# A two-layer kernel whose second layer begins inside the first layer's plan, with its first transfers planned and another table of due times

## The chip, the cores and the metric

One Trainium2 chip, one of its cores. The metric is the device time of one launch in microseconds (us). The kernel before ran three times: 2150.53, 2154.84 and 2156.69 us, median 2154.84.

## The reference

Both layers work on x of 32 sequences x 128 tokens x 512 numbers, in float32. Layer 0 is a cross attention with grouped heads (32 query heads of 16 numbers, 8 key and value heads) over a context, then a residual and a norm:

```python
q, k, v = hidden @ Wq + bq, context @ Wk + bk, context @ Wv + bv
scores = einsum("bkgld,bksd->bkgls", q, k) * scale + mask
out = einsum("bkgls,bksd->bkgld", softmax(scores), v)
x = out @ Wo + bo + hidden
x = (x - mean(x)) * rsqrt(var(x) + EPS) * gamma + beta
```

Layer 1 is a recurrent layer: its inputs are mixtures of each token with the one before (the first with a row of the context), its decay depends on the data, and its state of 16 x 16 numbers per head runs along the tokens:

```python
xn = ln(x); sx = token_shift(xn, state[:, 1])
xxx = tanh((xn + sx * maa_x) @ maa_w1)              # five parts of 32
x5 = xn + sx * (maa_stack + xxx @ maa_w2)           # w, k, v, r, g
w = exp(-exp(time_decay + tanh(x5[w] @ decay_w1) @ decay_w2))
r, k, v, g = x5[r] @ Wr.T, x5[k] @ Wk.T, x5[v] @ Wv.T, silu(x5[g] @ Wg.T)
for each token: out = r . (u * k v + s);  s = k v + w * s
att = head_norm(out) * gn_w + gn_b
x = x + att * g @ Wo.T
xn2 = ln(x); xk, xr = xn2 + sx2 * ffn_maa_k, xn2 + sx2 * ffn_maa_r
x = x + sigmoid(xr @ fWr.T) * (square(relu(xk @ fWk.T)) @ fWv.T)
```

## The kernel before

**Groups.** Each layer goes through the 32 sequences in 16 groups of two. Layer 0 has one function for a group, attend. Layer 1 has four: load1 (the group's rows and its start state), front (norm, mixtures, projections), recurrence (the scan along the tokens) and tail (the output projection and the feed-forward half). x between the layers goes through DRAM (x1d), in 256 KB tiles.

**The plan.** Nothing is issued in the order in which it is written. Each call of add makes a step: an engine, an estimate of its work, a function that issues its instructions, and the tiles (cells) that it reads and writes. A table (WHEN0 for layer 0, WHEN1 for layer 1) gives each kind of step a due time in units of groups; the step's due is its group plus that entry. give_out is a list scheduler: it models the engines' free times, and at each turn issues the step that can begin first and, among those that begin within 0.3 us, the one that is due first. A step may not run more than a set number of groups ahead of the oldest step that isn't issued (15.2739 in layer 0, 13.2672 in layer 1). A cell takes a place in a pool of few buffers at its first write; a place comes free when all uses of its cell are issued (`_places`). In layer 1 a further rule, turns, holds that the cells of one pool take their places in the order of their due times; in layer 0 it is off. What comes out is a fixed order for each engine: PE, DVE, ACT, POOL, and SP, whose queue carries most DMAs. Within an engine all is in order, DMA issues and their waits too.

**The two plans.** Layer 0's plan is given out in full; then the weights of layer 1 are loaded from ACT's queue (L726 to L763) and the constants made; then layer 1's plan begins, with pools of its own. The first transfers are outside the plan: ident and col, then on SP wk, wv, bk, ev, bv_bc, three row_bc and prev (L433 to L450), on ACT's queue wq and wo, all in the order of the program, ahead of the first x, ct and mask (L490 to L498).

**Layer 0, one group**, by the names of tiles: x is transposed (pxT L506, xT L512) and projected (pq L557); the context, loaded already transposed (ct), gives pk (L530) and pv (L583). Scores sc (L613), mask and softmax (pr L629, mx L641, exps L653), transposes ppT (L665) with copies pT (L670, L672), po (L677). The row sums go out to DRAM and come back spread over partitions (rs, rT, rd L701, bc L707), and scale oT (L711). pw (L716) is the output projection, then residual, norm and store of x1d (L719 to L724).

**Layer 1, one group.** load1 fetches x1t and s0 (L988). front: norm and transposes (zt L415, pxnt L860, xnt L868), the mixture xx (L905), ph0 (L924) and its tanh h0 (L1009); px5 (L1025) for two of five mixtures at a time, finished on DVE (L1041) and POOL (L1055); pdd (L1090), which needs the mixture w, with hd (L1095); pk and pv (L938), copied to kx and vx (L1071); v goes to DRAM (vd L1105) to be fetched spread (kv L1230); pr, pg, and the decay pew (L1162), ew (L1172). recurrence: POOL multiplies (L1252), DVE scans (a L1267) and multiplies by r (ar L1281), PE sums over the key index (acc L1296, pd L1207, pc L1321), and takes the variance pvar (L1344). tail: rstd (L1350) is spread by pb (L1357), pwo, the second norm with pxnc (L860), pkk, pkv, prr and the store. The feed-forward weights fk and fr are fetched anew for each group (L1400).

In PSUM, tiles of one bank (tag g) serve most of PE's results, three places in each layer. pdd's instructions, which pack four products of 32 rows, stand in one step:

```python
        for c in range(KC):
            for i, w, src in ((0, wd1[:, c, 0:32], xw), (1, wd1[:, c, 32:64], xw),
                              (2, w1[:, c, P:160], xx), (3, w1[:, c, P:160], xx)):
                nc.tensor.matmul(pdd()[32 * i : 32 * i + 32, :N], w, flat(src()[:, c]), ...)
```

The main loop issues nothing; it fills the plan: front of group 0, then for each group front of the next, recurrence, tail.

Of the kernel before, what the change touches and what calls it, by code (L numbers as in the profile page):

```python
# [8 lines left out]
F32 = mybir.dt.float32  # L9
# [5 lines left out]
P = 128  # L15
B = 32
# [19 lines left out]
        oT 0: -2.6252, oT 1: 3.3357, pT 0 0 0: -0.1744, pT 0 1 0: 1.2267, pT 1 0 0: -1.9192, pT 1 1 0: -0.8740,  # L36
        pr 0 0 0 0: 0.6529, pr 0 0 0 1: -0.0746, pr 0 0 1 0: -4.0682, pr 0 0 1 1: -0.1561, pr 0 1 0 0: 0.4501,
        pr 0 1 0 1: -0.3203, pr 0 1 1 0: -0.7878, pr 0 1 1 1: 0.0820, pr 1 0 0 0: 1.7871, pr 1 0 0 1: 2.2002,
        pr 1 0 1 0: -0.8730, pr 1 0 1 1: -1.8966, pr 1 1 0 0: -0.4270, pr 1 1 0 1: -2.0592, pr 1 1 1 0: 3.7724,
        pr 1 1 1 1: -0.8531, qT 0: -0.5042, qT 1: -0.0255, qT 2: -0.2635, qT 3: -1.0961, xT 0: 0.4768, xT 1: -0.1677  # L40
    """,
    "DVE": """
        kT 0: 1.2690, kT 1: -3.2473, mx 0 0 0: -1.1417, mx 0 0 1: -0.2864, mx 0 1 0: 1.2620, mx 0 1 1: -2.6166,
        mx 1 0 0: 2.6711, mx 1 0 1: -0.5335, mx 1 1 0: 1.7226, mx 1 1 1: -0.3724, pT 0 0 1: -1.2967, pT 0 0 2: 0.0513,
        pT 0 0 3: 0.0848, pT 0 1 1: -8.6724, pT 0 1 2: 0.0095, pT 0 1 3: -0.9150, pT 1 0 1: 0.2278, pT 1 0 2: 1.5335,
        pT 1 0 3: 0.1265, pT 1 1 1: -0.6521, pT 1 1 2: 0.0264, pT 1 1 3: -1.1512, pprev: -0.5247, pr 0 0 0: 3.0552,
        pr 0 0 1: -0.2034, pr 0 1 0: -6.8992, pr 0 1 1: 0.0841, pr 1 0 0: 3.8180, pr 1 0 1: 5.4106, pr 1 1 0: -0.1859,
        pr 1 1 1: -1.0387, pv: 1.4494, rT 0: 1.7614, rT 1: -6.4827, rs 0: 0.0025, rs 1: -1.3038, st a 0: 3.4819,
        st a 1: -0.7930, x 0: -1.6215, x 1: -0.7745
    """,  # L50
    "PE": """
        pk: -1.2090, po 0 0: -0.9547, po 0 1: -1.2559, po 1 0: 1.2553, po 1 1: -6.5573, ppT 0 0 0: -3.2574,
        ppT 0 0 1: -3.1897, ppT 0 0 2: 0.0759, ppT 0 0 3: -0.0050, ppT 0 1 0: -5.1850, ppT 0 1 1: -1.0390,
        ppT 0 1 2: -1.3378, ppT 0 1 3: -0.1908, ppT 1 0 0: -0.7659, ppT 1 0 1: 0.2863, ppT 1 0 2: -2.6538,
        ppT 1 0 3: -0.7327, ppT 1 1 0: -1.0396, ppT 1 1 1: -1.1030, ppT 1 1 2: -1.7141, ppT 1 1 3: -1.3304,
        pprev: 0.5587, pq 0: -0.5900, pq 2: -0.5203, pv: -0.7591, pw 0: -0.0622, pw 1: 0.0036, pxT 0: -1.1551,
        pxT 1: -1.2087, sc 0 0: -0.4025, sc 0 1: -0.1903, sc 1 0: 0.0128, sc 1 1: 0.3141
    """,
    "POOL": """
        oT 0: 1.2881, oT 1: 3.1556, sd a 0: -1.3405, sd a 1: -6.4837, x 0: -1.9469, x 1: 2.5134, z 0: -5.8626,  # L60
        z 1: -2.1882
    """,
    "SP": """
        bc 0: -0.4187, bc 1: -0.5237, ct 0: -1.3394, ct 1: -1.7142, m 0: -0.3457, m 1: 0.1999, rd 0: -8.2177,
        rd 1: 2.2127, x 0: -1.7606, x 1: -2.6917, z 0: 0.8576, z 1: -0.5330
# [4 lines left out]
        att 0: 8.9413, att 1: 10.3245, att 2: 10.9514, att 3: 4.2202, ew 0: 3.0530, ew 1: 7.1294, ew 2: 5.4799,  # L70
        ew 3: -0.1804, gt 0: 2.7896, gt 2: 7.2564, h0: 4.2793, hd: -0.7228, kk 0: 1.5652, kk 2: 8.9401,
        kv 0 0 0: 2.8237, kv 0 0 1: 2.8350, kv 0 1 0: 6.5988, kv 0 1 1: 4.7931, kv 1 0 0: 11.5248, kv 1 0 1: 12.1370,
        kv 1 1 0: 8.1713, kv 1 1 1: 8.4770, kv 2 0 0: 11.3074, kv 2 0 1: 0.7816, kv 2 1 0: 10.6862, kv 2 1 1: 7.1872,
        kv 3 0 0: 19.3264, kv 3 0 1: 5.1004, kv 3 1 0: 5.3317, kv 3 1 1: 6.5296, pk 0: 7.8527, pk 2: 3.7734,
        pv 0: 2.8655, pv 2: 13.4147, r 0: 10.0348, r 2: -0.1824, rr 0: 13.0999, rr 1: 2.8864, rstd: 5.6019,
        sq 0: -0.0986, sq 1: 8.8327, sq 2: 0.5974, sq 3: 5.6588, w4 0: 6.7771, w4 1: 3.1835, w4 2: 6.2518,
        w4 3: 1.3276, xnc 0: 5.1909, xnc 1: 3.5402, xnc 2: 5.5512, xnc 3: 9.4093, xnt 0: 4.3436, xnt 1: 6.3722,
        xnt 2: 7.1367, xnt 3: 8.6670, xx 0: 11.9355, xx 1: 6.5413, xx 2: 5.6875, xx 3: 9.8818, yk 0: 11.1356,
        yk 1: 1.7804, yk 2: 15.8112, yk 3: 13.9956, yr 0: 7.4657, yr 1: 8.8095, yr 2: 3.2938, yr 3: 8.7878,
        zc 0: 7.6581, zc 1: 0.9023, zt 0: 10.9657, zt 1: 5.2637  # L80
    """,
    "DVE": """
        a 0 0: -0.5883, a 0 1: -0.2414, a 0 2: 0.1043, a 0 3: 8.0118, a 1 0: 7.0047, a 1 1: 12.1762, a 1 2: 5.6912,
        a 1 3: 9.0685, a 2 0: 9.3322, a 2 1: 6.5083, a 2 2: 6.9110, a 2 3: 0.9712, a 3 0: 7.3177, a 3 1: 7.6874,
        a 3 2: 2.3097, a 3 3: 12.5406, ar 0 0: 2.4656, ar 0 1: 9.7666, ar 0 2: 5.7906, ar 0 3: 7.9178, ar 1 0: 6.6300,
        ar 1 1: 1.2202, ar 1 2: 6.5895, ar 1 3: 8.7855, ar 2 0: 28.3612, ar 2 1: 16.5392, ar 2 2: 12.3754,
        ar 2 3: 11.7973, ar 3 0: 9.1129, ar 3 1: 12.3189, ar 3 2: 9.0665, ar 3 3: 1.8400, gn 0: 8.4672, gn 1: 5.8193,
        gn 2: 3.6790, gn 3: 6.5194, gt 0: 0.0430, gt 2: -0.3529, own 0: 7.8602, own 1: 10.0300, own 2: 6.6987,
        own 3: 5.2960, pb 0: 0.7953, pb 1: 8.4093, pb 2: 4.1923, pb 3: 8.8563, raw 0: 2.2489, raw 1: 0.4033,
        raw 2: 5.9725, raw 3: 6.8204, rk 0: -0.4021, rk 1: 1.1444, rr 0: 7.1091, rr 1: 5.2378, rstd: 2.3485,  # L90
        st c 0: 6.9368, st c 1: 1.2521, st t 0: 8.7646, st t 1: 7.8543, x1c 0: 1.0294, x1c 1: 6.6954, x5 0 0: 2.9930,
        x5 0 1: 7.2539, x5 0 2: -1.0976, x5 0 3: 11.6924, x5 1 0: 8.4707, x5 1 1: -0.2943, x5 1 2: 10.2532,
        x5 1 3: 6.3221, x5 2 0: -0.6575, x5 2 1: 6.4713, x5 2 2: 12.8297, x5 2 3: 15.9903, x5 3 0: 6.5967,
        x5 3 1: 6.3600, x5 3 2: -0.8402, x5 3 3: -0.6696, x5 4 0: 8.4589, x5 4 1: 12.8956, x5 4 2: -0.4045,
        x5 4 3: 5.3981
    """,
    "PE": """
        acc 0: 13.3710, acc 1: 6.5427, acc 2: 6.5657, acc 3: 5.8187, pb 0: 18.0159, pb 2: 13.4697, pc 0: 0.6934,
        pc 1: 3.6234, pc 2: 5.2455, pc 3: 6.5762, pd 0: 1.0255, pd 1: 5.0703, pd 2: 6.9998, pd 3: 6.9286, pdd: 8.4674,
        pew 0: 6.2963, pew 2: 8.3876, pg 0: 1.2658, pg 2: 11.7555, ph0: 5.5651, pk 0: -0.5984, pk 2: -0.5853,  # L100
        pkk 0: 6.0318, pkk 2: 6.3700, pkv 0: 3.8400, pkv 1: 1.5996, pr 0: 0.4302, pr 2: -0.2452, prr 0: 3.2418,
        prr 1: 6.5661, pv 0: 20.6763, pv 2: -0.4713, pvar: 9.0706, pwo 0: 6.3422, pwo 1: 7.2520, px5 1 0: 6.5332,
# [226 lines left out]
def xattn_rwkv_kernel(  # L329
# [91 lines left out]
    with ExitStack() as sa:  # L421
# [8 lines left out]
        for tag in ("ln_st", "ln_mv", "ln_sd"):  # L430
            pl.tag(tag, 2)
# [1093 lines left out]
```

## Time and profile before

| what | us |
|---|---|
| median of three runs | 2154.84 |
| the profiled execution | 2150.95 |
| its span | 2149.2 |
| PE busy, in the span | 1992.6 |
| one steady group of layer 0 (between two pxT) | 35.72 |
| one steady group of layer 1 (between two pk) | 88.7 |
| last pvar to the end | 56.8 |

Busy times are sums over instructions; the four compute engines and the DMA queues run side by side, tied by semaphores, so a share of 93% says that PE works nearly always, not that it works at full clock. The granted clock of PE, 0.962 of full in the mean, is given for each stretch. The costliest groups of instructions (line, engine, operation, tiles; busy time, mean ns of one; idle time of the engine before them and what ended most of it):

```profile
L1252 POOL TENSOR_TENSOR kv<-kv,kx 128x1016 f32<-128x1016 f32 x256 | 597.6, 2349 | 142.9 <-DMA kv<-vd 63.1
L1267 DVE TENSOR_TENSOR_SCAN a<-w,kv 128x1024 f32<-128x1024 f32 x256 | 587.3, 2294 | 29.1 <-ACT w L1191 8.0
L653 ACT ACTIVATE pr<-pr,mx 128x128 f32<-128x128 f32 x1024 | 398.3, 391 | 53.4 <-DVE mx L641 47.0
L1281 DVE TENSOR_TENSOR ar<-a,r 128x1024 f32<-128x1024 f32 x256 | 311.5, 1217 | 4.4
```

### The profile page before, as it was taken

Reading aid. Unit: us, or ns where it says so; the run is one execution under the profiler, and the core shown is the slowest. Engines: PE = TensorE matmul, PEld = TensorE weight load, DVE = VectorE, ACT = ScalarE, POOL = GpSimd, SP = SyncE. Lnnn points to the kernel's source line nnn. Section 1 sums busy time; section 2 is a strip of 40 time slices with the busy share of each in tenths; the row PEclk is TensorE's granted clock in tenths of the full one; section 3 lists DMA queues with packets and bytes.
Section 4 is the critical chain, followed back from the end, with each engine's and each line's share of the span. In section 5 each row is a group of like instructions: output and inputs, shape, how many; then the busy total and the mean of one; then the engine's idle time right before and its main releaser. Section 6 shows DMA issues by size and latency. Waiting matters only on the chain.

```text
span 2149.2 us, 36169 instructions
## 1 busy us (share of the span) xinstructions
PE 1992.6 (93%) x11908; PEld 1305.8 (61%) x11908; DVE 1783.0 (83%) x2182; ACT 1058.0 (49%) x3473; POOL 1294.0 (60%) x1081
## 2 busy tenths in 40 slices
PE   5999999999958779999999999999999999999977
PEld 4666666666626546566675665656657566575643
DVE  3888888888844888989988899898988989888881
ACT  3888888888842233433434434344343443433332
POOL 1273334343345666777777777777777877777552
PEclk9999999999978889999999999999999999999988
DMA  7232221221024687887977978879788797886851
GB/s 207 61 127 66 62 70 60 68 61 60 27 81 80 114 121 114 146 158 122 175 122 138 167 117 168 130 138 163 120 161 134 141 165 117 162 136 115 163 99 59
DMA packets 155883, 252.23 MB, mean 117 GB/s; under 512 B 50512, under 2 KB 97648, under 8 KB 139312
## 3 DMA queue, kind: packets, MB, share of 16 engines
q1 hardware_dynamic: 149232, 240.27, 59.8%
q10 hardware_dynamic: 6464, 9.66, 1.4%
q8 instruction: 94, 1.54, 0.4%
q14 instruction: 93, 0.76, 0.1%
HBM read 224.12 MB, written 25.69 MB: 116 GB/s over the span
## 4 chain that ended last, share of the span: by engine, by line
PE 52%; DVE 7%; ACT 2%; DMA 1%; issue 1%; POOL 0%; SPq 0%; POOLq 0%; DVEq 0%; ACTq 0%
PE pkk L938 5%; PE pwo L956 5%; PE pk L938 5%; PE pv L938 5%; PE pr L938 4%; PE acc L1296 4%; PE pkv L956 4%; PE pg L938 4%; PE prr L956 4%; DVE a L1267 3%; PE pdd L1090 2%; PE px L1025 2%; DVE x L1041 2%; PE pc L1321 1%; PE pew L1162 1%
## 5 line engine op out<-in xcount | busy, mean ns | idle before, releaser
L1252 POOL TENSOR_TENSOR kv<-kv,kx 128x1016 f32<-128x1016 f32 x256 | 597.6, 2349 | 142.9 <-DMA kv<-vd 63.1
L1267 DVE TENSOR_TENSOR_SCAN a<-w,kv 128x1024 f32<-128x1024 f32 x256 | 587.3, 2294 | 29.1 <-ACT w L1191 8.0
L653 ACT ACTIVATE pr<-pr,mx 128x128 f32<-128x128 f32 x1024 | 398.3, 391 | 53.4 <-DVE mx L641 47.0
L1281 DVE TENSOR_TENSOR ar<-a,r 128x1024 f32<-128x1024 f32 x256 | 311.5, 1217 | 4.4
L1055 POOL TENSOR_TENSOR x<-x,xnt 128x512 f32<-128x512 f32 x160 | 187.2, 1181 | 92.1 <-DVE x L1041 79.4
L653 ACT ACTIVATION_READ_ACCUMULATOR pr<-pr,mx 128x1 f32 x1024 | 193.7, 189 | 0.0
L1041 DVE SCALAR_TENSOR_TENSOR x<-px,col,sxt 128x256 f32<-128x256 f32 x320 | 133.9, 473 | 59.5 <-PE pdd L1090 37.2
L629 DVE TENSOR_TENSOR pr<-sc,m 128x1024 f32<-128x1024 f32 x128 | 153.7, 1210 | 32.1 <-PE sc L613 29.0
L665 PE MATMUL ppT<-ident,pr 128*128 128x128 f32 x1024 | 154.3, 281 | 12.1 <-DVE pT L672 4.3
L665 PEld LDWEIGHTS ppT<-ident,pr 128*128 128x128 f32 x1024 | 115.4, 141 | 77.9 <-issue 25.9
L641 DVE TENSOR_REDUCE mx<-pr 128x8 f32<-128x1024 f32 x128 | 155.5, 1215 | 2.7
L1296 PE MATMUL acc<-ar,give 128*32 128x256 f32 x2048 | 142.5, 394 | 12.6 <-DVE ar L1281 12.6
L672 DVE COPY pT<-ppT 128x512 f32<-128x512 f32 x192 | 128.3, 682 | 22.9 <-PE ppT L665 18.2
L397 POOL TENSOR_SCALAR sd_a<-mv_a 128x1 f32<-128x1 f32 x32 | 7.1, 223 | 214.6 <-DVE mv_a L393 214.5
L716 PE MATMUL pw<-wo,oT 128*128 128x512 f32 x256 | 122.3, 610 | 9.8 <-POOL oT L711 8.8
L938 PE MATMUL pkk<-yk,fk 128*128 128x256 f32 x512 | 121.4, 392 | 6.2 <-POOL yk L905 6.2
L956 PE MATMUL pwo<-wo,gt 128*128 128x512 f32 x256 | 122.2, 612 | 5.0 <-ACT xnt L868 2.9
L938 PE MATMUL pr<-x,wr 128*128 128x256 f32 x512 | 122.0, 387 | 3.8 <-DVE x L1041 3.8
L557 PE MATMUL pq<-xT,wq 128*128 128x256 f32 x512 | 122.9, 389 | 0.7 <-ACT xT L512 0.7
L938 PE MATMUL pk<-x,wk 128*128 128x256 f32 x512 | 123.3, 390 | 0.0
L956 PE MATMUL pkv<-fv,kk 128*128 128x512 f32 x256 | 120.3, 603 | 0.0
L938 PE MATMUL pg<-x,wg 128*128 128x256 f32 x512 | 117.6, 383 | 2.9 <-DVE x L1041 2.9
(146 smaller groups left out, 3714.7 us busy)
## 6 DMA issues: line engine op xcount, KB each, us to landing
kv<-vd SPq DMA_DIRECT2D x1024, 128.0 KB
fk<-in_fWkT_dram SPq DMA_DIRECT2D x16, 1024.0 KB
fr<-in_fWrT_dram SPq DMA_DIRECT2D x16, 1024.0 KB
x<-in_x_dram SPq DMA_DIRECT2D x32, 256.0 KB
ct<-in_ctxT_dram SPq DMA_DIRECT2D x32, 256.0 KB
bc<-rd SPq DMA_DIRECT2D x256, 32.0 KB
x1d<-z SPq DMA_DIRECT2D x32, 256.0 KB
x1t<-x1d SPq DMA_DIRECT2D x32, 256.0 KB
```

The source lines that it names most:

```text
L629: lambda b=b, sc=sc, jp=jp, pr=pr: nc.vector.tensor_tensor(pr(), sc()[:, 2 * jp : 2 * jp + 2].rearrange("p j g e s -> p (j g e) s"), ms[b] ...
L641: lambda pr=pr, mx=mx: nc.vector.tensor_reduce(mx(), pr(), AX.X, ALU.max, negate=True),
L653: nc.scalar.activation(pr()[:, 4 * i + h, :], pr()[:, 4 * i + h, :], AF.Exp, bias=mx()[:, 4 * i + h : 4 * i + h + 1], accum_out=sm()[:, h0 ...
L665: nc.tensor.transpose(pt()[:, h, :], pr()[:, 4 * i + h, :], ident)
L938: nc.tensor.matmul(pp()[:, i], (w() if isinstance(w, Cell) else w)[:, kc, (c + i) * P : (c + i + 1) * P], flat(src()[:, kc]), start=(kc == 0),
L956: nc.tensor.matmul(pp(), src()[:, c, b, :], (w() if isinstance(w, Cell) else w)[:, c, :], start=(c == 0), stop=(c == KC - 1),)
L1041: lambda i=i, c=c, pp=pp, half=half: nc.vector.scalar_tensor_tensor(flat(ts[i]()[:, c]), pp()[:, half], col[:, MS0 + i, c : c + 1], flat(s ...
L1055: lambda i=i, c2=c2: nc.gpsimd.tensor_add(ts[i]()[:, c2 : c2 + 2].rearrange("p c b t -> p (c b) t"), ts[i]()[:, c2 : c2 + 2].rearrange("p ...
L1252: lambda c=c, kv=kv, e=e: nc.gpsimd.tensor_tensor(kv()[:, e, :, :, 1:T], kv()[:, e, :, :, 1:T], k()[:, c, :, 0 : T - 1].unsqueeze(1).broad ...
L1267: lambda kv=kv, a=a, e=e: nc.vector.tensor_tensor_scan(a().rearrange("p j b t -> p (j b t)"), w4().rearrange("p j b t -> p (j b t)"), kv() ...
L1281: lambda c=c, a=a, ar=ar: nc.vector.tensor_tensor(ar(), a().rearrange("p j b t -> p j (b t)"), flat(r()[:, c]).unsqueeze(1).broadcast_to([ ...
L1296: nc.tensor.matmul(acc()[32 * j : 32 * j + 32, :N], give[:, d].rearrange("p e h -> p (e h)"), tiles[d]()[:, j], start=(d == 0), stop=(d == 3),
```

## The change

The same tiles are computed by the same instructions; where they stand, and in which queues, changes.

1. **One table more than before, none the same.** Both tables are replaced, entry by entry, and so are the bounds on running ahead: 15.2739 becomes 9.8213 in layer 0, 13.2672 becomes 0.7291 in layer 1. Layer 0's table now holds the names of layer 1's front too. add takes a due time that stands where the table has none.
2. **Layer 1's plan is made first,** with the pools that both layers can use (xt, s0, z, xn, sx, x5, h0, hd, the norms' small tiles and the one-bank PSUM tiles g), and layer 0's plan takes them in: ct now lies in sx, prev in z.
3. **front becomes a generator** that stops after hd. For the first group, load1 and that first part of front are put into layer 0's plan; the rest is taken up at the start of layer 1's.
4. **The first transfers are steps of the plan on SP:** wk, wv, wo (before on ACT's queue), bk and ev, bv, row_bc, prev, and as one step w1, wd1, w2, wd2 (before on ACT's queue).
5. **The rule of turns** no longer holds for the one-bank tiles g.
6. **Wv and Wg of layer 1** are reordered through one staging tile of 512 columns in eight steps, before through three of 1024 in four.
7. give_out forgets cells of the plan before whose uses are all issued, and sets the ends of what remains to 3.4.

```diff
+    FREE = ("g",)
-        s.due = s.group + self.when[s.key]
+        s.due = s.group + self.when.get(s.key, due - s.group)
-        if self.turns and any(c.turn - self.begun[c.tag] >= taken[c.tag] for c in fresh):
+        if self.turns and any(c.tag not in self.FREE and c.turn - self.begun[c.tag] >= taken[c.tag] for c in fresh):
     def give_out(self):
+        for _, _, live in self.pools.values():
+            live[:] = [c for c in live if any(u.end is None for _, _, u in c.uses)]
+            for c in live:
+                for _, _, u in c.uses:
+                    u.end = u.end and 3.4
...
+    pl1 = Plan(ctx, tc, WHEN1, 0.7291)
...
-        wt = sa.enter_context(tc.tile_pool(name="wt", bufs=3))
-        pl = Plan(sa, tc, WHEN0, 15.2739)
+        wt = sa.enter_context(tc.tile_pool(name="wt", bufs=1))
+        pl = Plan(sa, tc, WHEN0, 9.8213)
         pl.turns = False
+        pl.pools.update(pl1.pools)
...
         wq = load_w(Wq, E, "wq", wa, nc.scalar)
-        wk = load_w(Wk, P, "wk", wa, nc.sync)
-        wv = load_w(Wv, P, "wv", wa, nc.sync)
-        wo = load_w(Wo0, E, "wo", wa, nc.scalar)
+        def later(name, t, move, go, due):
+            c = Cell(None, None, name, t=t)
+            pl.add("SP", 0.5, go, w=[c], of=f"{name}_0", due=due, move=move)
+            return c
+        def weight(w, width, name, due):
+            t = wa.tile([P, KC, width], F32, name=name)
+            return t, later(name, t, width / 85, lambda: nc.sync.dma_start(t, w.rearrange("(c p) m -> p c m", p=P)), due)
+        wk, wk_c = weight(Wk, P, "wk", -0.9)
+        wv, wv_c = weight(Wv, P, "wv", -0.7)
+        wo, wo_c = weight(Wo0, E, "wo", -0.2)
...
+        bk_c = later("bk", bk_sb, 0.2, small, -0.85)
+        bv_c = later("bv", bv_bc, 0.4, lambda: nc.sync.dma_start(bv_bc, bv.broadcast_to([P, P])), -0.65)
+        row_c = later("rows", row_bc, 4.0, three, -0.1)
+        prev_c = pl.cell("z", [T, E], "prev_0")
+        pl.add("SP", 0.5, lambda: nc.sync.dma_start(prev_c()[: 2 * B], prev), w=[prev_c], due=0.5, move=0.7)
...
-            ct = pl.cell("ct", [P, KC, G, T], f"ct_{gr}")
+            ct = pl.cell("sx", [P, KC, G, T], f"ct_{gr}")
...
         for gr in range(NG):
             attend(gr)
+        w1_c = later("w1", w1, 5.0, first_weights, 2.0)
+        add, cell = pl.add, pl.cell
+        first = load1(0, NG - 2.0)
+        first.w = [w1_c]
+        ahead = front(first, NG - 1.5)
+        next(ahead)
         with tc.manual_schedule():
             pl.give_out()
...
-            for half in range(2):
-                tmp = wt.tile([P, 2, E], F32, tag="wtmp", name=f"wtmp_{n}{half}")
...
+            for c in range(KC):
+                tmp = wt.tile([P, E], F32, tag="wtmp", name=f"wtmp_{n}{c}")
+                nc.scalar.dma_start(tmp, src[c * P : (c + 1) * P])
...
         add("ACT", act(N), lambda: nc.scalar.activation(hd(), pdd()[:, :N], AF.Tanh), r=[pdd], w=[hd], due=D + 0.35)
+        yield
```

In the changed kernel's order of instructions the following stand differently around the steps named above. On SP: ident, col, wk, x_0_0, bk, ev, x_0_1, ct_0, the rows and contexts of groups 1 and 2, m_0_0, row_bc, and then wv, s0, bv, wo, prev, w1 and the rest. On PE, at the end of layer 0: ph0 of layer 1's first group before the last two po, px5 (w and k) on both sides of the last po, then pdd, the last pw, and pk. In layer 1, per group, between the second half of px5 (w and k) and pdd: half of pg, two pxnc and one pd.

## The prediction

> **What bounds the kernel now.** I read the busy shares first, then the 40 slices, then what each engine waited for, then single stretches of time.
>
> ```profile
> span 2149.2 us, 36169 instructions
> PE 1992.6 (93%) x11908; PEld 1305.8 (61%) x11908; DVE 1783.0 (83%) x2182; ACT 1058.0 (49%) x3473; POOL 1294.0 (60%) x1081
> PE   5999999999958779999999999999999999999977
> PEclk9999999999978889999999999999999999999988
> PE 52%; DVE 7%; ACT 2%; DMA 1%; issue 1%; POOL 0%; SPq 0%; POOLq 0%; DVEq 0%; ACTq 0%
> ```
>
> PE is busy 93% of the span and holds the chain that ended last. The slices show the exceptions: the first, and three or four around the twelfth (some 610 to 750 us), where the layers meet. Only there, and in PE's waits inside a group, is there anything to win. The table of PE's waits (us in total, times, longest):
>
> ```profile
> PE pdd L1090 <- DVE x L1041: 29.8, 14, 2.1
> PE pprev L471 <- DMA prev_sb<-in_prev_dram: 16.4, 1, 16.4
> PE pxnt L860 <- ACT zt L415: 13.8, 2, 13.2
> PE acc L1296 <- DVE ar L1281: 12.6, 6, 3.3
> PE ph L924 <- POOL xx L905: 8.9, 2, 5.3
> PE pw L716 <- POOL oT L711: 8.8, 3, 6.8
> ```
>
> One wait recurs (pdd, 14 of 16 groups); one belongs to the start; three belong to the meeting of the layers. That meeting on PE's timeline (start, duration, then in brackets the idle time before):
>
> ```profile
> 611.96 1.07 PE L677 MATMUL po<-pT,v 128*32 128x256 f32 x16
> 619.83 6.53 PE L716 MATMUL pw<-wo,oT 128*128 128x512 f32 x8 [6.80 <-POOL oT L711]
> 639.55 0.48 PE L860 MATMUL pxnt<-ident,zt 128*128 128x128 f32 x1 [13.19 <-ACT zt L415]
> 646.03 3.67 PE L924 MATMUL ph<-xx,w 128*128 128x256 f32 x8 [3.63 <-POOL xx L905]
> 661.76 2.43 PE L938 MATMUL pk<-x,wk 128*128 128x256 f32 x10
> ```
>
> From the end of the last po (613.0) to layer 1's first key projection pass 48.7 us in which PE does little. Stretches in windows (start:end, length, busy of PE, PEld, DVE, ACT, POOL, then the granted clock, the DMA share, GB/s): a steady layer 0 group, a steady layer 1 group, and four single microseconds after a pdd wait.
>
> ```profile
> 300.48:336.20 35.72, 35.52 (x274) 24.53 (x273) 31.71 (x47) 30.91 (x141) 13.54 (x17) 1.00 0.23 67
> 660.00:775.00 115.00, 93.89 (x510) 68.08 (x506) 81.35 (x90) 29.36 (x70) 71.75 (x51) 0.88 0.74 119
> 917.00:1006.00 89.00, 86.55 (x475) 56.10 (x474) 79.73 (x90) 35.03 (x77) 66.32 (x51) 0.98 0.82 143
> 1257.00:1258.00 1.00, 0.83 (x9) 0.46 (x12) 1.00 (x2) 0.38 (x1) 1.00 (x2) 0.51 1.23 246
> 1258.00:1259.00 1.00, 1.00 (x16) 0.60 (x12) 0.15 (x1) 0.00 (x0) 1.00 (x1) 0.50 1.12 148
> 1259.00:1260.00 1.00, 1.00 (x16) 0.53 (x12) 0.00 (x0) 0.00 (x0) 0.54 (x1) 0.50 1.04 131
> 1260.00:1261.00 1.00, 1.00 (x11) 0.38 (x4) 0.21 (x1) 0.22 (x1) 0.00 (x0) 0.78 1.04 131
> ```
>
> A layer 0 group takes 35.72 us and PE works 35.5 of them: nothing to win. A layer 1 group takes 88.7 us (starts of pk at 917.29, 1005.86, 1094.51, 1183.21, 1271.93). Its pdd waits 2.12 us, and then the clock is at half for 3.5 us, so that pdd takes 3.45 us (32 matmuls, 634 ns each) where the one at 722.45, without that wait, had 376 to 390 ns each, about 1.73. The wait costs 2.12 + 1.73 = 3.85 us a group. With .22 lost at pwo and .75 at a stretched pb (1.45 for .70), a layer 1 group without waits is 88.7 - 4.8 = 83.9 us.
>
> **The change part by part.** The sum is made against the profiled execution, 2150.95 us (span 2149.2); the three runs' median is 3.9 above it.
>
> *Start.* On SP x_0 is issued at 11.76 us, behind wk, wv, bk, ev, bv_bc, three row_bc (3.77 us) and prev. In the changed order x_0_0 stands behind ident, col and wk alone, row_bc behind m_0_0, wv at place 21, wo (now on SP, off ACT's queue) at 25, prev at 27. All 16 prior loads are still issued; those that moved back are first used by pv (wv), pw (wo) and pprev, each now placed after work that doesn't need it. DMA share is .89 over the first 40 us, so the bytes in front matter: pxT (18.23) should come at 8 to 10, pq (21.46) at 10 to 11. From pq to the first sc it was 12.25 us (33.71), with pv's 1.8 between, which now comes later: 10.4, so sc at 20.4 to 21.4. Gain between 9 (wv or wo late) and 16 (pq at 8); I take 13.
>
> *Layer 0 carries work of layer 1.* The first group's transposes (8 records, 1.2 us), ph0 (1.8) and the px5 half (1.06) enter a PE that was full: +4. ACT (31 of 36 us busy) gets about 6 us more in all and SP two x1t loads and s0, spread over the last groups; POOL, 13.5 of 35.7 busy, hides its part. The order of layer 0 itself changes with its table: the same matmuls; I see one late sc per group (pr before it on DVE), 0.6 us or less if it shows at all. Without a row for it: -2 to +10 over 16 groups; I take 0.
>
> *Weights through one staging tile.* Wv and Wg of layer 1 pass through wt, which falls from three tiles of 1024 columns to one of 512. The issues are on ACT's queue, in front of its exps, and each but the first now waits for the one before to land and for POOL's copy (1.07 us). Before, only the fourth waited:
>
> ```profile
> L755 ACTq EVENT_SEMAPHORE  x1: 3984/3984/3984, 133.1 to 133.1; - x1
> ```
>
> Now seven issues can wait, beside 0 to 16 exps (.39 each) between them: the second and the fifth have next to none between and cost about 4 us, the others 0 to 3. ACT would stand 10 to 18 us where it stood 4; it has 4.8 us of slack a group, and the stops lie in about two groups. PE waits for what ACT has no slack for: bounds 0 and +14; I take +6.
>
> *Meeting of the layers.* Gone from between the last po and pk are the store and load of x1 (618.6 to 636), the norm, zt, pxnt, xx, ph0. What remains: the 6.8 us wait for oT (the chain rs, rT, rd out and back, oT is unchanged), partly filled by px5 (1.06) and pdd (1.73 to 3.45), then half of pw (3.5, at half clock 6.5), then pk: 6.8 + 3.5 = 10 to 14 after po's end. Gain 48.7 - 10 to 14 = 34 to 38; 36. If the cover fails (pdd waits for wd or x5 behind layer 0's last adds on POOL, 1.2 us each, four of them), 5 less.
>
> *Fill of layer 1.* Before: pk 661.8, first scan 688.1 (26.4 later), pvar 774.7. Now pk comes before its helpers: kx, vx and the pools must first be free, two memsets of vx (1.85 us together at 633.31) stand behind layer 0's last norm on POOL, and pv follows pk by some 14 us instead of 3.6, as both pk halves, px5, pew and a transpose precede it. The scan waits for pv, store and fetch (22.8 us from pv to scan): 14 + 22.8 = 36.8 after pk, 10.4 later than before. Bounds 0 (PE's work in front of pv is not lost, it is done earlier) to 14; I take 10, because DVE, 81 of 115 us busy here, starts late.
>
> *Steady layer 1 groups.* In the new order between the second px5 half and pdd stand half of pg (1.73), two pxnc (2 x .58) and a pd (.43): 3.3 us of cover where before only four transposes stood. The 2.12 wait goes, and with it the half clock. What is late next: pr's second half waits for a PSUM place until DVE has read px5_4, pb waits for rstd, pew behind it, pkv for its copy. By the durations of before I get .65 near pdd, .3 at pkv, 1.2 at pr, 1.7 at pb and pew, 3.85 at most, none long. So between 83.9 and 87.75; DVE, 79.4 of 88.7 and in order, gives slack but little, so I take 87.0: -1.7 a group, by 14 groups -24. Bounds: -67 (83.9) and the case on the other side below.
>
> A rule bears on this. The Trainium skill, "TensorE: Matmul & The Clock Gate", section "HAM oscillation — how this bites in real kernels", holds that the clock falls after PE-idle gaps above some 3.4 us; here 2.12 us of idle were followed by .50, so the row disagrees. By the page a wait of 2.12 costs 2.12, the floor would be 1.7 higher, the period 88.7 and the gain of this part nothing: about 2123. The row decides.
>
> *Tail.* 56.8 us after the last pvar. PE waits 1.74 us for fr (issued 2128.42, needed 2133.56). In the new order pkv (2 x 3.5) stands before prr and covers it, and no prr of group 14 is left: -1, bounds 0 and -2.
>
> Sum: 2150.95 - 13 + 4 + 0 + 6 - 36 + 10 - 24 - 1 = 2096.95. The runs lie .4 below to 5.7 above the profiled one; with half of the median's 3.9: **2099 us**.
>
> **The rivals.**
> - *A: the ends are won, the period stays at 88.7.* The waits that I count small add up to what went. For it: DVE is at 90% and its scans can't be moved; against: the waits are short, so no half clock. 2099 + 24 = 2123.
> - *B: the fill gives it back.* Layer 1 cannot begin scanning sooner than its weights, pools and DVE allow; PE's earlier start becomes idle time before the first acc. For it: DVE 81 of 115 and a first scan that depends on a DRAM round trip; against: PE's work is the bound. All of the 36 but 4 lost, period as forecast: 2099 + 32 = 2131; with A as well some 2155.
> - *C: slower.* A scan (2.30) or scan and ar (3.5) stands in DVE's queue in front of both the x5_4 that frees pr's place and of rstd; PE then waits over 2 us at pr and at pb in each group, and each is followed by the half clock: 83.9 + 1 + 2 x 3.85 = 92.6, +3.9 x 14 = +54. Net of the ends (-13 + 4 + 6 - 36 + 10 - 1 = -30): 2154.84 - 30 + 54 = 2179. It decides from a period of 90.9 on, where 14 x 2.2 eats the 30. For it: both waits are on DVE, in order. Against: in the order of instructions I find at most 1.2 at the one.
> - *D: layer 0's order costs 1 us a group*, +16 on A or the forecast: 2115 to 2139. PE has no slack there.
>
> **How the numbers follow.** The forecast (2080 to 2113) .45, faster still (a period under 85.7) .10, A with D .20, B .12, C .13. The measurement tells 0.3%, 6.5 us, from no change. Faster by more: all but C and a part of B, .85; within .03; slower .12. The range leaves out C and reaches over A, B and the bounds of the steady group and the start: 2054 to 2148.
>
> **What would show it.** First pxT before 10 us and sc near 21; last po to first pk 10 to 14 us; first scan about 37 after pk; pk to pk in layer 1 about 87, no 2 us wait at pdd, granted clock not at half there; ACT's stops at the staging tile 10 to 18 us; other layer 0 groups at 35.7; no wait for fr. Wrong if the period is above 90, if a layer 0 group is above 36.5, or if acc waits long for the first scans.

## The result and the profile after

The changed kernel took 2124.7 us (median of four runs, 2121.72 to 2126.37), the kernel before, on the same chip, 2155.77. The ratio is 0.985, 95% interval 0.984 to 0.987: 31 us faster, against 56 forecast: inside the range of 2054 to 2148, outside the forecast's own stretch of 2080 to 2113. The profiled execution took 2124.67 us, its span is 2122.9.

The page of the changed kernel: span, busy time, PE's and the clock's slices, and the chain that ended last.

```profile
span 2122.9 us, 36158 instructions
PE 1975.3 (93%) x11908; PEld 1280.5 (60%) x11908; DVE 1787.5 (84%) x2182; ACT 1048.4 (49%) x3473; POOL 1294.3 (61%) x1081
PE   6989999999988689999999999999999999999976
PEclk9999999999999799999999999999999999999997
PE 31%; DMA 16%; DVE 11%; SPq 5%; issue 1%; ACT 1%; POOL 0%; DVEq 0%; POOLq 0%; ACTq 0%
```

The dent where the layers meet is smaller, but a dent in the third slice (106 to 159 us) is new, where the kernel before shows 9. What PE waited for (us in total, times, longest):

```profile
PE acc L1386 <- DVE ar L1370: 25.1, 11, 3.9
PE pr L546 <- DVE x L653: 13.1, 14, 0.9
PE pxT L907 <- DMA x<-in_x_dram: 10.9, 1, 10.9
PE ph L532 <- DVE x1c L1483: 9.2, 13, 0.7
PE pb L1452 <- DVE gt L771: 8.2, 12, 0.7
PE pd L1290 <- DVE gt L771: 7.3, 13, 1.0
PE po L1086 <- ACT pT L1079: 6.5, 3, 4.9
PE ppT L1074 <- ACT pr L1062: 6.3, 3, 3.7
```

The wait of 2.1 us at pdd is gone; four short ones (pr, ph, pb, pd) recur in its place, 2.9 us a group. Two waits on ACT in layer 0, at po and ppT, have grown to 6.5 and 6.3 us (before .7 and .9). acc's wait has doubled, from 12.6 us: 17.1 us of it lie between the first pk and 777 us, in the fill, 6.6 at the end. The meeting of the layers on PE's timeline (start, duration, idle time before):

```profile
633.82 1.07 PE L1086 MATMUL po<-pT,v 128*32 128x256 f32 x16
...
639.96 0.64 PE L705 MATMUL pdd<-x,wd 128*32 128x256 f32 x2 [3.48 <-POOL x L668]
...
643.27 3.70 PE L1127 MATMUL pw<-wo,oT 128*128 128x512 f32 x8
646.81 3.62 PE L546 MATMUL pk<-x,wk 128*128 128x256 f32 x16
```

From the last po matmul's start (634.51) to the first pk 12.3 us pass, 49.1 before. Windows of a steady layer 0 group, the fill of layer 1, and a steady layer 1 group (columns as in the prediction: the busy time of PE, PEld, DVE, ACT and POOL, then the granted clock, DMA share, GB/s):

```profile
301.40:337.30 35.90, 35.03 (x273) 24.02 (x272) 31.58 (x47) 30.73 (x141) 13.31 (x17) 1.00 0.22 65
646.80:768.00 121.20, 93.67 (x485) 64.83 (x483) 82.26 (x95) 29.82 (x70) 74.91 (x59) 0.82 0.73 116
1066.64:1154.17 87.53, 84.67 (x476) 54.31 (x472) 79.36 (x90) 34.87 (x78) 65.83 (x51) 1.00 0.85 145
```

A layer 1 group now takes 87.53 us at full clock. The span by stages, between the same marks on PE in both traces:

| stretch | before | after | change | term of the sum |
|---|---|---|---|---|
| start to the first sc | 33.71 | 24.68 | -9.0 | -13 |
| first sc of group 0 to that of group 1 | 32.43 | 41.71 | +9.3 | none |
| group 1 to group 5 | 149.50 | 164.65 | +15.1 | +6 (staging tile) |
| group 5 to group 15 | 357.25 | 358.87 | +1.6 | 0 |
| first sc of group 15 to the last po | 39.76 | 44.59 | +4.8 | +4 |
| last po to the first pk of layer 1 | 49.11 | 12.30 | -36.8 | -36 |
| first pk to the first pvar | 112.98 | 121.20 | +8.2 | +10 |
| first pvar to the last | 1317.62 | 1298.87 | -18.8 | -24 |
| last pvar to the end | 56.81 | 56.01 | -0.8 | -1 |
| span | 2149.16 | 2122.89 | -26.3 | -54 |

The two large gains are there, near their size. The start's gain is lost within one group, and four groups of layer 0 lose more than half of the rest.

**Where layer 0 lost it.** ACT's timeline has two stops at a DMA issue in its own queue:

```profile
36.93 0.28 ACTq L1169 DMA_DIRECT2D wo<-in_WoT_dram  x1
37.26 0.40 ACT L1062 ACTIVATE pr<-pr,mx 128x128 f32<-128x128 f32 x1 [5.66 <-DMA s<-in_s_dram]
...
123.60 0.38 ACTq L1178 DMA_DIRECT2D wtmp_v<-in_WvT_dram  x1
124.02 0.59 ACT L1079 COPY pT<-ppT 128x512 f32<-128x512 f32 x1 [7.57 <-POOL sd_t L412]
```

At 36.93 an issue of wo1 waited for the landing of s0, a transfer that it has nothing to do with but a semaphore in common (both carry number 100 in the trace), and the exps of the first group waited behind it, 5.66 us. At 123.60 the second load into the staging tile was issued, after two waits: one for a semaphore, begun at 117.3 (the longest of the line's seven, 3471 ns), then one for POOL's copy of the first load. POOL was at something else:

```profile
L1178 ACTq EVENT_SEMAPHORE  x7: 17/38/3471, 117.3 to 158.3; - x7
116.69 5.90 POOL L1186 TENSOR_SCALAR wo<-wo 128x512 f32<-128x512 f32 x4
122.53 1.04 POOL L1179 COPY wv<-wtmp_v 128x512 f32<-128x512 f32 x1
```

The copy of 1.04 us stood behind four scalings of wo1. But the first load had landed at 117.32, and up to 120.81 ACT waited for a fetch of layer 0's row sums (rd) that the second load shares a semaphore with, number 104; only the 2.8 us from there to 123.60 are due to the copy behind the scalings. In all ACT stood 7.57 us, and PE's po behind it 4.90; from 124.1 us on the clock was at half for 6.8 us as well.

### The profile page after: what moved, and what is told of

Same layout as the page of the kernel before. It is cut to its first block, busy times and chain, and to the rows that moved or that the text cites. A ratio compares the mean times of both kernels' runs of the same rounds, so it can differ in the third digit from the quotient of the medians.

```text
span 2122.9 us, 36158 instructions
## 1 busy us (share of the span) xinstructions
PE 1975.3 (93%) x11908; PEld 1280.5 (60%) x11908; DVE 1787.5 (84%) x2182; ACT 1048.4 (49%) x3473; POOL 1294.3 (61%) x1081
## 3 DMA queue, kind: packets, MB, share of 16 engines
q8 instruction: 94, 1.54, 0.4%
## 4 chain that ended last, share of the span: by engine, by line
PE 31%; DMA 16%; DVE 11%; SPq 5%; issue 1%; ACT 1%; POOL 0%; DVEq 0%; POOLq 0%; ACTq 0%
DMA kv<-vd 16%; PE pk L546 5%; PE pkk L546 5%; DVE a L1355 5%; SPq L721 3%; PE pwo L564 3%; PE px L637 3%; PE acc L1386 3%; PE pg L546 2%; DVE ar L1370 2%; PE pv L546 2%; PE pkv L564 2%; SPq L1316 2%; PE pdd L705 1%; PE ph L532 1%
## 5 line engine op out<-in xcount | busy, mean ns | idle before, releaser
L653 DVE SCALAR_TENSOR_TENSOR x<-px,col,sxt 128x256 f32<-128x256 f32 x320 | 134.6, 474 | 36.5 <-PE px L637 34.2
L1074 PEld LDWEIGHTS ppT<-ident,pr 128*128 128x128 f32 x1024 | 114.6, 142 | 76.7 <-ACT pr L1062 30.4
L546 PE MATMUL pg<-x,wg 128*128 128x256 f32 x512 | 122.8, 388 | 0.5 <-ACT att L1421 0.4
L546 PE MATMUL pv<-x,wv 128*128 128x256 f32 x512 | 120.1, 383 | 1.2 <-ACT xnt L472 1.2
L564 PE MATMUL prr<-fr,yr 128*128 128x512 f32 x256 | 119.3, 599 | 0.7 <-ACT rr L1529 0.7
L546 PEld LDWEIGHTS pr<-x,wr 128*128 128x128 f32 x512 | 97.5, 193 | 34.7 <-DVE x L653 19.9
```

The source lines that it names most:

```text
L546: nc.tensor.matmul(pp()[:, i], (w() if isinstance(w, Cell) else w)[:, kc, (c + i) * P : (c + i + 1) * P], flat(src()[:, kc]), start=(kc == 0),
L564: nc.tensor.matmul(pp(), src()[:, c, b, :], (w() if isinstance(w, Cell) else w)[:, c, :], start=(c == 0), stop=(c == KC - 1),)
L653: lambda i=i, c=c, pp=pp, half=half: nc.vector.scalar_tensor_tensor(flat(ts[i]()[:, c]), pp()[:, half], col[:, MS0 + i, c : c + 1], flat(s ...
L1074: nc.tensor.transpose(pt()[:, h, :], pr()[:, 4 * i + h, :], ident)
```

## The experiments

The experiments ran on three chips, on which the kernel before had medians of 2153.41 to 2159.48 us. Each ratio is to the kernel before on the same chip; stretches come from one profiled execution each.

**1. The new table alone.** The kernel before, with layer 1's new table, its bound, and g free of the rule of turns.

```diff
-    pl = Plan(ctx, tc, WHEN1, 13.2672)
+    pl = Plan(ctx, tc, WHEN1, 0.7291)
-        if self.turns and any(c.turn - self.begun[c.tag] >= taken[c.tag] for c in fresh):
+        if self.turns and any(c.tag != "g" and c.turn - self.begun[c.tag] >= taken[c.tag] for c in fresh):
```

> The kernel before, with nothing but layer 1's new table, its bound of 0.7291 and the one-bank tiles freed from the rule of turns. My theory: the steady groups of layer 1 are set by the table alone, so the spacing of pk falls from 88.7 to 87.5 us as in the changed kernel, there is no 2 us wait at pdd and no half clock, and the total falls by the 18.75 us that the changed kernel gained between its first and last pvar (1317.6 to 1298.9), give or take 5 for another fill: 2132 to 2142. Rival: the period came from the other parts (pools shared with layer 0, the start in another phase); then pk stays at 88.7 and the time within 5 us of before.

2131.24 us, ratio 0.990 (0.987 to 0.992). Groups of 87.53 us, first to last pvar 1299.3, no wait of 2 us at pdd. The theory holds (the time is .8 below its range): these three edits, none of which touches layer 0, bring 24 of the 31 us. The bound and the freed g were not tried apart from the table. (The changed kernel has two tables, as the kernel before, not one more.)

**2. The rest alone.** The changed kernel with layer 1's old table, bound and rule.

```diff
-    FREE = ("g",)
+    FREE = ()
-    pl1 = Plan(ctx, tc, WHEN1, 0.7291)
+    pl1 = Plan(ctx, tc, WHEN1, 13.2672)
```

> The changed kernel with layer 1's old table, bound 13.2672 and rule of turns. My theory: layer 0, the meeting of the layers and the start stay as in the changed kernel, and layer 1 goes back to 88.7 us a group with the 2 us wait at pdd: 2125 + 19 = 2144, between 2137 and 2150. Rival: the meeting gains only because the new table fills it (pk right after the last pw); then the old table loses that as well and the time is above 2155.

2154.99 us, ratio 1.001 (0.999 to 1.002): no change against before, and 5 us above the range of my theory. The meeting is won here too (17.3 us instead of 49.1, not 12.3), so the rival's cause is wrong, but layer 0 loses it again, the fill takes 125.2, and layer 1's steady groups run from 88.3 to 91.1 (the profiled execution, at 2160.74, is one of the longer ones). So all parts but the table are together worth nothing with the old table, and some 7 us on top of the new one (2131.24 to 2124.7).

**3. The staging loads on SP.**

```diff
-                nc.scalar.dma_start(tmp, src[c * P : (c + 1) * P])
+                nc.sync.dma_start(tmp, src[c * P : (c + 1) * P])
```

> The changed kernel with the eight loads of the staging tile issued from SP's queue instead of ACT's. My theory: between the first sc of layer 0's second group and that of its sixth the changed kernel lost 15.1 us against before (164.6 for 149.5), because ACT stood behind those issues; without them there the stretch falls to 150 to 155 and the time by 10 to 15 us, to 2110 to 2115. Rival: the stretch is lost to layer 0's new order and to the weights' bytes; then it stays at 160 or more and the time within 4 us of 2125. Or SP's queue now stands behind POOL's copies and the contexts come late: above 2125.

2122.78 us, ratio 0.985 (0.983 to 0.987). The stretch from the second to the sixth group falls from 164.65 to 153.65, as expected: ACT stood behind the staging loads there. But the first group takes 51.3 us instead of 41.7, since ACT now stands 13.8 us at another issue of wo1, and the total hardly moves. The stop had another place, not an end.

```profile
ACT qT L975 <- DMA wo<-in_WoT_dram: 13.8, 1, 13.8
```

**4. ACT's queue freed.** All that comes after wr1 is issued from SP: wo1, the staging loads, fv, rows3, gcol, same, back_n.

```diff
-            nc.scalar.dma_start(
+            nc.sync.dma_start(
                 wo1[d * HC : (d + 1) * HC], WoT.rearrange("(c h d) m -> d h c m", h=HC, d=S)[d]
...
-        fv = load_w(fWvT, E, "fv", cp, nc.scalar)
+        fv = load_w(fWvT, E, "fv", cp, nc.sync)
```

> The changed kernel with all of layer 1's late weights (wo1, the staging loads, fv, rows3, gcol, same, back_n) issued from SP instead of ACT's queue; only wq, wk1 and wr1 stay there. My theory: this also takes away the 5.66 us for which ACT stood before its second set of exps, at an issue of wo1 that waited for s0 to land; the first sc of the second group comes at 57 to 61 us instead of 66.4, the stretch to the sixth group is 150 to 155, and the time is 2103 to 2112, lower than with the staging loads alone. Rival: SP's queue is now what is late (some 55 more issues in front of x, ct and the row sums), DVE waits for masks and PE for oT, and the time is 2120 or more.

2113.69 us, ratio 0.981 (0.979 to 0.983). The first sc of the second group comes at 59.95 us, as expected; the four groups after it take 156.5 and the time is 2 us above the range, both a little more than the theory has, but far from the rival's. What is left of PE's waits in those groups is mostly one on POOL:

```profile
PE pw L1127 <- POOL oT L1122: 7.0, 2, 4.7
```

**5. The wait at pdd filled with work,** in the kernel before.

```diff
         def hidden():
+            for c in range(KC):
+                nc.tensor.matmul(pdd()[:, :N], w1[:, c, 0:P], flat(xx()[:, c]), start=True, stop=True)
             for c in range(KC):
```

> The kernel before, with four matmuls put ahead of pdd's own in the same step, whose results pdd's first matmuls overwrite (added work, 1.7 us at full clock, ready long before and so inside the 2.12 us for which PE waits). Price by the rows (wait, then half clock): PE doesn't idle, the half clock after it goes, and each group gets 1.6 to 1.7 us shorter though it does more: pk to pk 87.0 to 87.1 instead of 88.74, total 2155 - 14 x 1.65 = 2132, between 2126 and 2140. Rival (the clock falls only after some 3.4 us of idle, and what is slow here is pdd itself, with its 32 column tiles): pk to pk stays 88.7 and the time within 5 us of 2155. Second rival: the added work makes pdd late, and the time goes above 2160.

2183.07 us, ratio 1.012 (1.010 to 1.013). The experiment missed its aim: the added matmuls don't need the mixture, yet the wait stands in front of them as before (from 1000 to 1900 us, ten groups):

```profile
PE pdd L1084 <- DVE x L1041: 20.3, 10, 2.0
```

What the added work needs is pdd's place in PSUM; that the wait is for this place, which DVE's x frees, is what remains, though it was not tried by another place. The miss tells something else: in five groups running (pk to pk 88.96) the wait of 2.0 us was there and the clock stayed full; in others it fell. The time is that of the second rival, and it is what the added work costs when none of it is covered: 26 us for 16 x 1.7.

**6. The kernel before with .86 us more work a group.**

```diff
             def go(i=i):
+                if name.startswith("pkk") and i == 0:
+                    nc.tensor.matmul(pp()[:, 0], w()[:, 0, c * P : (c + 1) * P], flat(src()[:, 0]), start=True, stop=True)
                 for kc in range(KC):
```

> The kernel before, with two matmuls more per group of layer 1 (in pkk, repeated and overwritten by its own first ones; .43 us each, .86 a group). Before's pk to pk came to 88.74 us, which is 26 times the 3.413 us in which the clock's halves begin and last in its records, and its deviations from that halved from group to group (88.56, 88.65, 88.70, 88.72, 88.73). Theory: the half clock starts on that grid and hits pdd; a group that comes later loses less to it, so the period is held at 26 x 3.413; added work of .86 costs nothing in the steady groups: pk to pk stays 88.74, total 2155 to 2160. Rival: PE is simply the bound, each group costs .86 more, pk to pk 89.6, total 2155 + 16 x .86 = 2169.

2163.43 us, ratio 1.003 (1.002 to 1.004), between the theories: 6.5 us for 13.8 us of work. The steady groups don't keep 88.74 but go mostly in pairs, 87.99 and 89.45 in turn, whose mean is 88.72, as before without the work. The rows of pdd in two neighbouring groups (after the start, each line's duration):

```profile
1172.53 0.64 PE L1092 MATMUL pdd<-x,wd 128*32 128x256 f32 x2 [2.13 <-DVE x L1043]
1172.54 0.64 PE L1092 MATMUL pdd<-xx,w 128*32 128x256 f32 x2
...
1261.98 0.41 PE L1092 MATMUL pdd<-x,wd 128*32 128x256 f32 x2 [2.13 <-DVE x L1043]
1261.99 0.41 PE L1092 MATMUL pdd<-xx,w 128*32 128x256 f32 x2
```

The same wait, 2.13 us in both; after the first one pdd runs at half clock, after the second at full. The granted clock of these two stretches:

```profile
1172.50:1175.90 3.40, 3.37 (x33) 1.62 (x33) 1.01 (x1) 0.24 (x1) 2.39 (x2) 0.55 1.10 178
1261.98:1265.40 3.42, 3.42 (x52) 1.93 (x52) 2.38 (x4) 1.45 (x4) 2.37 (x2) 1.00 1.00 168
```

A group without half clock takes 87.99 with the added .86, so before's own order would take 87.1 without it. Its own trace has such a group: the wait of 2.13 us that ended at 904.12 was not followed by half clock, and from pk to pk it took 87.14.

**7. The same work in the changed kernel,** by the same edit.

> The same two matmuls more per group, in the changed kernel, whose layer 1 shows no half clock between 777 and 2060 us. Theory: nothing holds its period, so pk to pk goes from 87.53 to 88.2 to 88.4 us (PE is the bound in 84.7 of 87.5 us) and the time from 2125 to 2134 to 2139. Rival: the period is set by DVE's chain (79.4 us busy, and PE's waits on it), the work fills PE's waits, and pk to pk stays below 87.8, the time below 2129.

2135.83 us against 2124.7 for the changed kernel (its ratio to before is 0.990, 0.989 to 0.992). Groups of 88.39 us against 87.53: in the steady groups the .86 is paid in full; 11 us in all. Nothing holds this kernel's period, and PE's work sets it.

**8. The scalings out of layer 0.** On top of the freed queue, wo1 and fv are halved by steps of layer 1's plan.

```diff
-        for w in (wo1, fv):
-            for c in range(KC):
-                nc.gpsimd.tensor_scalar_mul(w[:, c], w[:, c], 0.5)
...
+    for w in (wo1_c, fv_c):
+        for c in range(KC):
+            add("POOL", 1.47, lambda w=w, c=c: nc.gpsimd.tensor_scalar_mul(w()[:, c], w()[:, c], 0.5),
+                w=[w], of=f"half{w.name}_0_{c}", due=-0.5 + 0.1 * c)
```

> As the kernel with ACT's queue freed, and the eight scalings of wo1 and fv (1.47 us each on POOL) taken out of layer 0's third and fourth group and put as steps into layer 1's plan, where POOL waits for the first state products. Theory: POOL's scalings stand in front of oT and so of pw (7.0 us of PE's waits in the kernel with the queue freed); without them the first sc of the sixth group comes 149 to 153 us after that of the second (156.5 with them), and the time is 2106 to 2111. Rival: the scalings are now in front of the first kv in the fill, first scan later by up to 12 us, and the time is 2113 or more.

2112.25 us, ratio 0.979 (0.978 to 0.980): 156.3 us from the second group to the sixth, where 149 to 153 were expected. The theory is wrong: POOL's scalings are not what costs the time in front of oT (6.6 us of PE's waits are left there). The first scan isn't later either.

**9. The new table and the freed queue, without the early front.** Experiment 1's kernel with the same weights on SP; here the staging has its three tiles.

> The kernel before with layer 1's new table, bound and free one-bank tiles, and with layer 1's late weights (wo1, staging loads in four through three tiles, fv, rows3, gcol, same, back_n) on SP instead of ACT's queue; no planned first transfers, no front of layer 1 inside layer 0. Theory: the queue matters only where the staging tile is single, so layer 0 gains little here (149.5 to 151 us from the second to the sixth group's first sc falls by 0 to 4), the meeting of the layers stays at 49 us, and the time is 2126 to 2132 against 2131 for the table alone; what the early front brings is then the rest to 2112, some 15 to 19. Rival: the freed queue is what brought the 10 us, in any kernel; then the time is 2118 to 2123 and the early front is worth less than 10.

2129.25 us, ratio 0.990 (0.988 to 0.992), as the theory has it: the freed queue is worth 2 us here by the times and nothing by the ratios (experiment 1 has 0.990 too), so it can't be told from nothing. Experiment 4, with the same queue and all of the change, stands at 0.981: the rest of the change, the early front and the planned transfers with the single staging tile and layer 0's new table, is worth some 16 us (2113.69; 19 by the ratios) once ACT's queue is out of its way. Its parts were not tried one by one.

**10. s0 later,** on top of experiment 8: the loads of s0 for the first group are added to the plan after front's yield, and left out of load1 (not shown).

```diff
         yield
+        for b in range(0 if gr else G):
+            g.states(b)
         g.k, g.v = kx[gr % 2], vx[gr % 2]
...
```

> As the kernel with the scalings late, and the first group's start states (s0) loaded by layer 1's plan rather than among the first transfers. Theory: s0's small pieces no longer share the DMA engines with the first contexts and masks, and the first sc of the second group comes 32 to 34.5 us after the first (35.85), the time is 2108 to 2111. Rival: after the queue was freed nothing waits for s0, the stretch stays within .7 of 35.85 and the time within 3 of 2112.

2113.87 us, ratio 0.982 (0.980 to 0.984); the first group takes 35.87 us, unchanged. s0 matters only through an issue on ACT's queue that waits for it; with that gone no cost is seen.

**11. No staging tile,** on top of experiment 8.

```diff
+        for src, dst, tmp in ((WvT, wv1, wo1), (WgT, wg1, fv)):
+            nc.sync.dma_start(tmp, src.rearrange("(c p) m -> p c m", p=P))
...
-                tmp = wt.tile([P, E], F32, tag="wtmp", name=f"wtmp_{n}{c}")
```

> As the kernel with the scalings late, without a staging tile: Wv is loaded whole into the tile of wo1 and Wg into that of fv, eight copies on POOL reorder them, and then wo1 and fv get their own weights, all on SP. Theory: what layer 0 still loses from its second to its sixth group (156.3 us between their first sc, four periods of 35.9 are 143.6) comes from the single staging tile, whose loads and copies one after the other stand in front of the row sums on SP and of oT on POOL (6.6 us of PE's waits); without it the stretch is 145 to 150 and the time 2101 to 2107. Rival: it is the other weights' issues on SP (34 for rows3 and gcol), and the stretch stays above 153, the time above 2109; or SP waits for the copies early and the first group loses it (first to second sc above 38).

2104.74 us, ratio 0.975 (0.973 to 0.976), the fastest of all. From the second to the sixth group 147.7 us, as expected, and the wait for oT isn't in the list any more. In experiment 8 SP stood 7.7 us (longest 6.6) at issues into the staging tile until POOL's copy of wv was done; these waits are gone too. So the single tile was the cost, by its order: eight loads and copies one after the other. That there are now two loads in place of eight, and that wo1 and fv come later, was not tried apart from it.

**12. The constants back on ACT's queue,** on top of experiment 11.

```diff
-            nc.sync.dma_start(rows3[at], by_d[:, 32:35, :])
+            nc.scalar.dma_start(rows3[at], by_d[:, 32:35, :])
...
```

> As the kernel without the staging tile, with rows3, gcol, same and back_n issued from ACT's queue again, as in the changed kernel. Theory: these issues wait for no copy; ACT (31 of 36 us busy in a group) pays their 0.3 us each, some 10 us over one or two groups, and half of it reaches PE: 3 to 6 us above the kernel without the staging tile. Rival: SP's queue is what is late then, and the time falls by 2 to 4 against it.

2112.07 us, ratio 0.978 (0.976 to 0.980): 7.3 us worse, but not as expected. The four later groups are the best of all (145.6); the first takes 43.7, because ACT stands at its own issues again, for s0 and the weights (5.4 and 5.2 us) and for rows3 (4.6). What costs is the landing that an issue waits for, not the 0.3 us of the issue.

## Why the prediction was right

The direction and the range held; of the gain, 54 in the sum, 26.3 of the span came. The difference of 27.7 us, by the table: first group 9.3, staging 9.1, layer 1's groups 5.2, start 4.0, layer 0's order 1.6, inserted work .8, tail .2, less 1.8 by which the fill and .8 by which the meeting came out better. That the time lies in the range owes much to the range's width; the rivals A and A with D are nearer to it than the forecast. Two of the signs of being wrong showed: layer 0 groups above 36.5 us (45.06 and 44.05, at the staging tile; the kernel before has up to 38.43), and acc's long waits in the fill.

- *Meeting of the layers* (-36, came -36.8), *inserted work* (+4, +4.8), *tail* (-1, -0.8): near what was worked out. The cover failed in part: pdd waited 3.48 us for POOL's x and then ran at half clock to 643.3, .9 us past the end of oT; the rest lay inside the wait for oT that was there anyway.
- *Fill* (+10, came +8.2): near by luck in part. The first scan came 44.5 us after pk instead of 36.8: PE waited 2.70 for kx and the second pk ran at half clock (6.58 us). From the first scan to the first pvar it then took 76.7 us, 86.6 before, which I hadn't counted on.
- *Start* (-13, came -9.0): the first pxT at 10.87 us, not before 10. Then the term lacks its second half: I costed the moved issues up to the first sc and not what else the earlier work would meet. The first group's exps came while ACT's queue was still full of wo1's issues, one of which waited for s0, a transfer that the change brings to the front of SP's queue (the prediction has it spread over the last groups). Half clock for 6.8 us followed. Of the 9.3 us that the first group lost, 5.8 are gone in experiment 4, whose ACT queue is free (35.87 us); 3.4 are left, and their cause stays open. In the profiles of experiments 2 and 7, whose layer 0 is the same, the stretch is 38.73 and 38.33, so the stop's size varies. The step that failed is the sentence that the moved loads cost nothing because their users come later: the queue that they were moved past was counted, the issues on another queue that wait for their landing weren't.
- *Staging tile* (+6 between 0 and 14, came +15.1): the mechanism was right (seven waits, ACT ahead of the exps, PE behind it), the size wasn't. ACT's idle gaps that hold an issue into the tile add up to 16.0 us (7.57, 1.10, 4.82, 1.54 and .96; the trace puts the end of three of them down to PE or DVE), inside the 10 to 18 forecast; what I sized too small is what of them reaches PE. I left out the half clock that followed (10.2 us of it in two places between 124 and 165 us) and, for the longest stop, both the landing of a fetch with the same semaphore (3.5 us) and what stands before the copy on POOL. Experiment 3 moved 11 of the 15 out of there; in experiment 11, without the tile, the stretch is 147.7 us, below the 149.5 of before.
- *Steady groups of layer 1* (-1.7 each to 87.0, came -1.2 to 87.53). Of the waits that I called late next pr's (.9), pb's (.7) and one near pdd (pd, .5) came; ph's (.7) I hadn't named, and pew and pkv don't wait. Together they are 2.9 us, where I took 3.1. What was wrong is the floor: 84.7 of busy PE, not 83.9. Without the .75 that I took off for a stretched pb the sum gives 84.65. Rival A, whose time (2123) is nearest to the measured one, is not what happened: the period did fall, and the ends were given back in layer 0. D had the place right, layer 0, but not as a cost of each group: 1.6 us in ten groups.
- *What the half clock did.* I priced the wait at pdd at 2.12 + 1.73 in every group. Experiment 6 shows the same wait without the second part. By its rows before's order takes 87.1 us a group without half clock, and the new order 87.53: the new table doesn't wait less (2.9 us in four pieces for 2.3 in two), it waits in pieces that the clock doesn't answer. Its gain is the half clock, less .4 us a group.

As for the rule weighed in the prediction: by the page the period would have stayed at 88.7, and it fell, so the row was the better guide; but experiments 5 and 6 show that the row isn't a rule either.

The Trainium skill, "TensorE: Matmul & The Clock Gate", section "What's actually happening", says that the gate decides in free-running windows of 3413 ns and knows two states; the records here agree, with every half clock of a trace beginning on one grid of 3.413 us and, but for the one that the kernel's end falls into, lasting a multiple of it.

## What to carry to other kernels

A DMA issue in a compute engine's queue makes that engine wait for whatever the issue waits for: a buffer, a copy on another engine, even the landing of a stranger's transfer. Before moving a load earlier, list which issues on every queue come to stand behind it, and keep issues that can wait off an engine that is busy 85% of the time. An early start is worth only as much as the next shared resource lets through: here of the 9 us of the start and the 37 us at the meeting some 7 were left in the whole, and the rest paid only when ACT's queue was freed and the staging tile taken out (2124.7 to 2104.7 us, on another chip; ratio .985 to .975). And where a recurring wait is followed by a lower clock, as here, short waits in its place can be cheaper though their sum is larger (2.9 us for 2.3).

## What the runs showed of the hardware

**A wait's price depends on its place on a grid.** In the kernel before, half clock in layer 1's steady groups begins every 88.74 us, which is 26 times 3.413; pk to pk there is 88.56, 88.65, 88.70, 88.72, 88.73, 88.74, each half as far from 88.74 as the last. The explanation that fits, though no run shows it by itself: PE pays half of that part of the 3.413 us in which it works, so a group that comes a little late loses a little less. The period is then held at a multiple of the grid. Experiment 6 bears it out in part: .86 us more work, and the mean of two groups still 88.72, though in pairs and not steadily, as I had expected. In the kernels with the waits in pieces (experiments 1 and 7 and the changed one) nothing of the kind is seen, and in experiment 7 the added work is paid in full.

**When it falls.** Over the third to the fifteenth group of the kernel before and of experiments 5 and 6 (39 waits of 2.0 to 2.1 us) the half clock followed at the next border of the grid where 1.2 us or more of the wait lay before that border, or the wait lay whole between two; it did not follow where the wait lay across a border with 1.02 us or less before it. One wait with 1.04 us before the border was followed by it. This is a description of these 39 alone: in the changed kernel a wait of 2.16 us at ppT, 1.61 of it before the border (153.23 to 155.39), and one of 1.82 at pdd, whole between two borders (800.06 to 801.89), were not followed. So neither some 2 us of idle nor 3.4 is the threshold; what the gate counts was not settled.
